# An edge-attention kernel: the edge and query projections laid out by edge instead of by feature and turned, with a looser tie of the gathers to TensorE

## The chip, the cores and the metric

The kernel runs on one core of one Trainium2 chip. The metric is the device time of one execution in microseconds (us). The parts of a core that matter here are TensorE (matrix products into PSUM, "PE" in the profile, its weight loads "PEld"), VectorE ("DVE"), ScalarE ("ACT"), GpSimd ("POOL", which here only issues indirect gathers), SyncE ("SP", which issues the plain DMAs) and the 16 DMA engines behind the queues.

## What is computed

A graph layer with 6,250 nodes of 128 features and 206,250 edges that are sorted by destination. With 8 heads of 16 features:

```python
Qh, Kh, Vh = h @ WQ, h @ WK, h @ WV          # per node, seen as (8, 16)
Eh = edge_attr @ WE                          # per edge
score = einsum('ehd,ehd,ehd->eh', Kh[src], Qh[dst], Eh) / 4
score = exp(clip(score, -5, 5))
wV = segment_sum(Vh[src] * score[:, :, None], dst)
Z = segment_sum(score, dst)
x = layernorm(x + wV / (Z[:, :, None] + 1e-06))
```

So each edge needs a product of three vectors (K of its source, Q of its destination, E of its own), a sum over each head's 16 features, an exponential, and a weighted V that is added into its destination.

## The kernel before

**Tiles and batches.** The edges are cut into 1,612 tiles of 128. A batch is four tiles (the last eight tiles make smaller ones), which gives 406 batches. A table of K and V by node (`kv`, 256 floats a row) and a table of Q (three bf16 parts of each row) are first written to DRAM by `table` and `q_rows`.

**What a batch does, engine by engine.**
- POOL gathers the rows of K and V of the batch's sources, one indirect DMA a tile (`gather`, line 307). The buffers are `kvrows`, GB = 17 of them.
- DVE makes two one-hot matrices (`stage_0`, line 337): `onehot` (edges on partitions, destination in a window on the free axis) for the final sum, and `onehotT` (126 rows of Q parts on partitions, edges on the free axis) to pick each edge's Q.
- PE picks Q with one bf16 product of 512 columns into `qps` (line 354). Features are then on partitions and edges on the free axis. ACT copies this to SBUF as `qT` (line 356). PE makes E in the same layout with one f32 product of 512 columns into `eps` (line 358); the profile counts an f32 product as two passes.
- DVE multiplies `qT` by `eps` into `eq` (`pairs`, line 365).
- PE turns the four 128x128 blocks of `eq` into `pps`, so that edges lie on partitions (`turn`, line 373).
- DVE multiplies the gathered K by `pps` (`kq`, line 379), sums over each head (`sc`, line 382) and clips (line 385). ACT takes the exponential twice, into a PSUM bank and into the last columns of `msg` (`weigh`, lines 391 and 393). DVE multiplies V by it (`messages`, line 413). PE adds the messages into `agg`, one f32 product a tile with `onehot` as the weights (`stage_c`, line 431). Every 11 tiles ACT copies `agg` to `sum` (line 441), and now and then PE joins the sums (`finish`), after which DVE norms a block of 128 nodes, one small instruction at each `fill()`.

**The order.** From batch 12 on the order of every engine is that of the program text (`manual_schedule`). In iteration b of the main loop (line 464) PE gets turn(b-1), the Q and E products of b, possibly a `finish`, and then agg(b-3). DVE gets kq, sc and clip of b-2, messages of b-3, the one-hots of b+2, and at the end `eq` of b. ACT gets qT(b), possibly `fin`, the exponentials of b-2, possibly `sum`.

**The tie.** POOL could run ahead as far as its buffers allow. From batch 16 on, line 318 makes the first gather of batch b wait for the Q product (`expanded`) of batch b - lag(b). The lag is 12 at batch 16 and falls by one every four batches down to STEP = 1 at batch 60. So later than that, gather(b) waits for the Q product of b-1.

**PSUM.** `eps` and `qps` have one bank each, `pps` two, `agg` two.

Of the kernel before, what the change touches and what calls it, by code (L numbers as in the profile page):

```python
# [8 lines left out]
F32 = mybir.dt.float32  # L9
I32 = mybir.dt.int32  # L10
BF16 = mybir.dt.bfloat16
AF = mybir.ActivationFunctionType
ALU = mybir.AluOpType
AX = mybir.AxisListType

P = 128
N, E, D, H, DH = 6250, 206250, 128, 8, 16
# [7 lines left out]
MW = D + H  # L25
B = 4
CH = 8
GB = 17
XB = 12
LOCK = XB + 4  # L30
STEP = 1
TAIL = 8
HEAD = 132
NG = (NT + G - 1) // G
AHEAD = 2
# [45 lines left out]
def edge_attention(ctx: ExitStack, tc: tile.TileContext, x, xT, srcT, dstT, dstB, dst0, bnd, lo, eaT,  # L81
# [30 lines left out]
    with ExitStack() as fast:  # L112
# [91 lines left out]
        ep = fast.enter_context(tc.tile_pool(name="edges", bufs=EB))  # L204
        wp = fast.enter_context(tc.tile_pool(name="work", bufs=3))
        sp = fast.enter_context(tc.tile_pool(name="sums", bufs=7))
        psE = fast.enter_context(tc.tile_pool(name="psE", bufs=1, space=bass.MemoryType.PSUM))
        psQ = fast.enter_context(tc.tile_pool(name="psQ", bufs=1, space=bass.MemoryType.PSUM))
        psP = fast.enter_context(tc.tile_pool(name="psP", bufs=2, space=bass.MemoryType.PSUM))
        psT = fast.enter_context(tc.tile_pool(name="psT", bufs=1, space=bass.MemoryType.PSUM))  # L210
        psA = fast.enter_context(tc.tile_pool(name="psA", bufs=2, space=bass.MemoryType.PSUM))
        psX = fast.enter_context(tc.tile_pool(name="psX", bufs=1, space=bass.MemoryType.PSUM))
# [1 line left out]
        bank = psX.tile([P, P + B * H], F32, name="bank")  # L214
        iota_p, exp_p = bank[:, :P], bank[:, P:].rearrange("p (b h) -> p b h", h=H)
        nc.vector.tensor_copy(iota_p, iota_f)

        def pair_bank(i, name, shape):

            pool, tag = ((psE, "eps"), (psP, "pps"), (psQ, "qps"), (psP, "pps"))[i % 4]  # L220
            return pool.tile(shape, F32, name=name, tag=tag)


        KB = 4
# [1 line left out]
        def table(b0):  # L226
            st = wp.tile([P, KB, 2 * D], F32, name="kvst", bufs=2)
            blocks = range(b0, min(NB, b0 + KB))
            for b in blocks:
                n = min(P, N - b * P)  # L230
                ps = pair_bank(b, "kvacc", [P, 2 * D])
                nc.tensor.matmul(ps[:n], xT_sb[:, LEFT + b * P:LEFT + b * P + n], wkv_sb,
                                 start=True, stop=True)
                if b % 2:
                    nc.vector.tensor_copy(st[:n, b - b0, :], ps[:n])
                else:
                    nc.scalar.copy(st[:n, b - b0, :], ps[:n])
            full = [b for b in blocks if (b + 1) * P <= N]
            if full:
                nc.sync.dma_start(  # L240
                    kv[b0 * P:(b0 + len(full)) * P].rearrange("(b p) f -> p b f", p=P),
                    st[:, :len(full), :])
            if len(full) < len(blocks):
                b = blocks[-1]
                nc.sync.dma_start(kv[b * P:N], st[:N - b * P, b - b0, :])
# [43 lines left out]
        def load_chunk(c):  # L289
            if c in chunks or c * CH >= NT:  # L290
                return
            n = min(CH, NT - c * CH) * P
            tl = ep.tile([P, CH * P], F32, name="ea")
            nc.sync.dma_start(tl[:, :n], eaT[:, c * CH * P:c * CH * P + n])
            chunks[c] = tl

        def ea_tiles(t, n):

            load_chunk(t // CH)
            j = t % CH * P  # L300
            return chunks[t // CH][:, j:j + n * P]

        def lag(b):

# [18 lines left out]
        def project(g, n):  # L323

            pt = psT.tile([P, B, P], F32, name="xtps", tag="oT")
            for i in range(n):
                nc.tensor.transpose(pt[:, i, :], g[:, i, :D], ident)
            xgT = wp.tile([P, B, P], F32, name="xgT", tag="kq", bufs=2)
            nc.scalar.copy(xgT[:, :n], pt[:, :n])
            for i in range(0, n, 2):  # L330
                k = min(2, n - i)
                pk = pair_bank(i // 2, "kvps", [P, 2, 2 * D])
                for j in range(k):
                    nc.tensor.matmul(pk[:, j, :], xgT[:, i + j, :], wkv_sb, start=True, stop=True)
                nc.scalar.copy(g[:, i:i + k, :], pk[:, :k, :])

        def stage_0(b):
            t0, n = batches[b][0], len(batches[b])
            oh = wp.tile([P, B, P], F32, name="onehot", bufs=AHEAD + 5)
            nc.vector.tensor_tensor(oh[:, :n], iota_p[:, None, :].to_broadcast([P, n, P]),  # L340
                                    rel[:, t0:t0 + n, None].to_broadcast([P, n, P]), op=ALU.is_equal)
            ohT = wp.tile([QROWS, B * P], BF16, name="onehotT", bufs=AHEAD + 2)
            e0 = t0 % RC * P
            nc.vector.tensor_scalar(ohT[:, :n * P], rels[t0 // RC][:, e0:e0 + n * P], node[:QROWS], None,  # L344
                                    op0=ALU.is_equal)
            st8[b] = oh, ohT

        def stage_a(b, g):
            t0, n = batches[b][0], len(batches[b])
            if b < XB:  # L350
                project(g, n)
            oh, ohT = st8.pop(b)
            pq = psQ.tile([P, B * P], F32, name="qps")
            expanded[b] = nc.tensor.matmul(pq[:, :n * P], loaded[t0 // WT], ohT[:, :n * P], start=True, stop=True)  # L354
            qT = wp.tile([P, B * P], F32, name="qT", bufs=2)
            nc.scalar.copy(qT[:, :n * P], pq[:, :n * P])  # L356
            pe = psE.tile([P, B * P], F32, name="eps")
            nc.tensor.matmul(pe[:, :n * P], we_sb, ea_tiles(t0, n), start=True, stop=True)  # L358
            st8[b] = [n, g, oh, pe, qT]

        def pairs(b):

            n, g, oh, pe, qT = st8[b]
            eq = wp.tile([P, B * P], F32, name="eq", bufs=2)
            nc.vector.tensor_tensor(eq[:, :n * P], qT[:, :n * P], pe[:, :n * P], op=ALU.mult)  # L365
            st8[b] = [n, g, oh, eq]

        def turn(b):

            n, g, oh, eq = st8[b]  # L370
            pp = psP.tile([P, B, D], F32, name="pps")
            for i in range(n):
                nc.tensor.transpose(pp[:, i, :], eq[:, i * P:i * P + P], ident)  # L373
            st8[b] = [n, g, oh, pp]

        def stage_b(b):
            n, g, oh, pp = st8[b]
            t1 = wp.tile([P, B, D], F32, name="kq", bufs=2)
            nc.vector.tensor_tensor(t1[:, :n], g[:, :n, :D], pp[:, :n], op=ALU.mult)  # L379
            fill()  # L380
            sc = wp.tile([P, B, H], F32, name="sc")
            nc.vector.tensor_reduce(sc[:, :n], t1[:, :n].rearrange("p b (h d) -> p b h d", h=H),  # L382
                                    axis=AX.X, op=ALU.add)
            fill()
            nc.vector.tensor_scalar(sc[:, :n], sc[:, :n], -20.0, 20.0, op0=ALU.max, op1=ALU.min)  # L385
            st8[b] = [n, g, oh, sc]

        def weigh(b):

            n, g, oh, sc = st8[b]  # L390
            nc.scalar.activation(exp_p[:, :n], sc[:, :n], AF.Exp, scale=0.25)  # L391
            m = wp.tile([P, B, MW], F32, name="msg")
            nc.scalar.activation(m[:, :n, D:], sc[:, :n], AF.Exp, scale=0.25)  # L393
            st8[b] = [n, g, oh, m]

# [62 lines left out]
        def fill():  # L458

            if norms and next(norms[0], None) is None:  # L460
                norms.pop(0)

        held = []
        for b in range(nbat + 4):
            if b >= XB and not manual:
                manual.append(fast.enter_context(tc.manual_schedule()))
            held += [(b + SLAG, store) for store in stores]
# [3 lines left out]
            if b < nbat:  # L471
                load_chunk(batches[b][0] // CH + EB - 3)
                load_rel(batches[b][0] // RC + 1)
                load_q(batches[b][0] // WT + QLOOK)
                g = gathered.pop(b) if b in gathered else gather(b)
                if b == min(XB, nbat - 1):
                    late_loads()
                if b == min(XB + 8, nbat - 1):
                    relative(C0, NT)
                if b == 14:  # L480
                    from_window(1)
                if b == 0:
                    for i in range(AHEAD):
                        stage_0(i)
                if b > 0:
                    turn(b - 1)
                stage_a(b, g)
            elif b == nbat:
                turn(b - 1)
            norms.extend(pending)  # L490
            pending.clear()
            for q in ready:
                finish(q)
            ready.clear()
            if 0 <= b - 2 < nbat:
                stage_b(b - 2)
            if 0 <= b - 3 < nbat:
                messages(b - 3)
            fill()
            if b + AHEAD < nbat:  # L500
                stage_0(b + AHEAD)
            if b < nbat:
                pairs(b)
            if 0 <= b - 2 < nbat:
                weigh(b - 2)
            if 0 <= b - 3 < nbat:
                stage_c(b - 3)
            fill()
            if b < nbat:
                while len(built) < q_built(min(NJ - 1, batches[b][0] // WT + QLOOK + 2)):  # L510
# [157 lines left out]
```

## Time and profile before

| | |
|---|---|
| runs | 2429.15, 2424.27, 2415.33 us; median 2424.27 |
| profiled execution | 2430.0 us, of which the traced span is 2428.1 us |
| TensorE clock granted, mean | 0.811 of full speed |
| busy: PE, PEld | 1539.8 us, 1086.0 us |
| busy: DVE | 1577.4 us |
| busy: ACT | 458.9 us |
| busy: POOL | 1534.0 us |
| DMA | 398.16 MB, mean 164 GB/s |
| chain that ended last | PE 34%, another core or an unknown queue 23%, DVE 19%, issue 16%, ACT 4% |

Busy time is the time in which an engine executes something; a row of the groups table gives the name of the tile that is written, what is read, the shapes, how often, the busy sum, the mean of one, and then the idle time of that engine just ahead of these instructions with the event that ended it. "issue" there is idle time for which the profile shows no wait. "remote", or "another core or an unknown queue", is a wait whose end the profile could not pair with an instruction. The starts of matmuls are recorded, their ends are modelled.

### The profile page before, as it was taken

What the parts mean: (1) busy time and instruction counts of PE and PEld (TensorE: products, weight loads), DVE (VectorE), ACT (ScalarE), POOL (GpSimd) and SP (SyncE); (2) the same over time, 40 slices, a digit from 0 to 9 for tenths busy, and PEclk for the clock granted to TensorE, in tenths of its full rate; (3) what the DMA queues carried; (4) which work ended last, traced back from release to release, by engine and by line L of the source; (5) the groups of instructions that cost most, each with busy time, mean ns of one, the idle gap of its engine ahead of it and who ended that gap; (6) DMA issues with size and microseconds to landing.
All of it is one profiled execution on the core that took longest, in us unless ns stands there. A gap on an engine that the chain in (4) does not pass through costs nothing.

```text
span 2428.1 us, 24930 instructions
## 1 busy us (share of the span) xinstructions
PE 1539.8 (63%) x6880; PEld 1086.0 (45%) x6880; DVE 1577.4 (65%) x3779; ACT 458.9 (19%) x1572; POOL 1534.0 (63%) x1619
## 2 busy tenths in 40 slices
PE   3587666666665666657666666666666656656665
PEld 2365444444444444444444444444444444444444
DVE  1368778666766666667667666666666667666766
ACT  0232122111111111111111111111111111111111
POOL 7346565666666666666666666666666666666664
PEclk6898898887878888778877878788778788887887
DMA  5645555556554555556456554655555556554642
GB/s 176 201 144 174 179 156 178 165 150 185 170 166 148 168 177 156 164 152 196 147 157 196 160 156 149 184 168 151 169 162 178 147 155 196 157 156 146 197 150 71
DMA packets 178482, 398.16 MB, mean 164 GB/s; under 512 B 61756, under 2 KB 87526, under 8 KB 178336
## 3 DMA queue, kind: packets, MB, share of 16 engines
q0 software_dynamic: 76592, 208.18, 29.4%
q1 hardware_dynamic: 100604, 187.38, 25.2%
q8 instruction: 57, 0.93, 0.2%
q10 hardware_dynamic: 1140, 0.93, 0.1%
q14 instruction: 89, 0.73, 0.1%
HBM read 381.54 MB, written 14.81 MB: 163 GB/s over the span
## 4 chain that ended last, share of the span: by engine, by line
PE 34%; another core or an unknown queue 23%; DVE 19%; issue 16%; ACT 4%; DMA 2%; POOL 1%; DVEq 1%; SPq 0%; ACTq 0%; POOLq 0%
PE agg L431 10%; PE eps L358 10%; PE pps L373 7%; DVE sc L382 4%; DVE kq L379 4%; DVE eq L365 3%; PE qps L354 3%; ACT qT L356 2%; DVE msg L413 2%; PE finps L401 2%; POOL kvrows L314 1%; DVE onehot L340 1%; DVE onehotT L344 1%; DMA kvrows<-kv,src 1%
## 5 line engine op out<-in xcount | busy, mean ns | idle before, releaser
L314 POOL DMA_INDIRECT kvrows<-kv,src x1564 | 1487.1, 951 | 862.3 <-issue 385.6
L431 PEld LDWEIGHTS agg<-msg,onehot 128*128 128x128 f32 x3224 | 516.7, 230 | 664.3 <-issue 520.9
L431 PE MATMUL agg<-msg,onehot 128*128 128x136 f32 x3224 | 560.5, 326 | 352.8 <-DVE msg L413 137.2
L373 PE MATMUL pps<-shift,eq 128*128 128x128 f32 x1612 | 320.5, 332 | 419.6 <-DVE eq L365 238.5
L365 DVE TENSOR_TENSOR eq<-qT,eps 128x512 f32<-128x512 f32 x406 | 276.4, 681 | 476.2 <-ACT qT L356 210.9
L358 PE MATMUL eps<-ea,we_sb 128*128 128x512 f32 (+1 forms) x812 | 528.2, 738 | 16.8 <-issue 13.4
L373 PEld LDWEIGHTS pps<-shift,eq 128*128 128x128 f32 x1612 | 221.4, 168 | 477.4 <-DVE eq L365 282.4
L356 ACT COPY qT<-qps 128x512 f32<-128x512 f32 x406 | 236.8, 583 | 1048.5 <-remote 428.8
L379 DVE TENSOR_TENSOR kq<-kvrows,pps 128x512 f32<-128x512 f32 x406 | 274.8, 677 | 12.1 <-remote 3.5
L413 DVE TENSOR_TENSOR msg<-kvrows,bank 128x512 f32<-128x512 f32 x406 | 274.6, 676 | 9.8 <-ACT bank L391 4.3
L382 DVE TENSOR_REDUCE sc<-kq 128x32 f32<-128x512 f32 x406 | 276.0, 680 | 7.3
L340 DVE TENSOR_TENSOR onehot<-bank,dst_sb 128x512 f32<-128x512 f32 x406 | 275.8, 680 | 0.0
L358 PEld LDWEIGHTS eps<-ea,we_sb 128*128 128x128 f32 x812 | 192.1, 238 | 50.0 <-issue 14.6
L354 PE MATMUL qps<-onehotT,qw 126*128 126x512 bf16 x406 | 187.3, 461 | 0.9 <-ACT qT L356 0.9
L344 DVE TENSOR_SCALAR onehotT<-relb,node 126x512 bf16<-126x512 bf16 x406 | 147.0, 363 | 16.7 <-remote 11.2
L391 ACT ACTIVATE bank<-sc 128x32 f32<-128x32 f32 x406 | 83.0, 204 | 257.2 <-DVE onehot L340 139.8
L401 PEld LDWEIGHTS finps<-sum,shift 128*128 128x128 f32 x478 | 73.1, 215 | 62.4 <-issue 33.9
L401 PE MATMUL finps<-sum,shift 128*128 128x136 f32 x478 | 75.8, 307 | 30.9 <-ACT sum L441 26.2
L262 DVE TENSOR_TENSOR qr<-qrows,qst 128x128 f32<-128x128 f32 (+1 forms) x49 | 14.2, 289 | 116.8 <-ACT qst L261 104.4
L393 ACT ACTIVATE msg<-sc 128x32 f32<-128x32 f32 x406 | 88.0, 217 | 0.0
L385 DVE TENSOR_SCALAR sc<-sc 128x32 f32<-128x32 f32 x406 | 79.2, 195 | 7.3
L441 ACT COPY sum<-agg 128x136 f32<-128x136 f32 x146 | 39.3, 269 | 236.2 <-remote 100.7
(66 smaller groups left out, 525.9 us busy)
## 6 DMA issues: line engine op xcount, KB each, us to landing
ea<-eaT SPq DMA_DIRECT2D x201, 512.0 KB
relb<-relD SPq DMA_DIRECT2D x100, 504.0 KB
kvrows<-kv,src POOLq DMA_INDIRECT x1564
qw<-qs SPq DMA_DIRECT2D x202, 31.5 KB
kv<-kvst SPq DMA_DIRECT2D x12, 512.0 KB
qs<-qst SPq DMA_DIRECT2D x48, 96.0 KB
xb<-x SPq DMA_DIRECT2D x48, 64.0 KB
out<-h SPq DMA_DIRECT2D x48, 64.0 KB
```

The costliest lines, as they stand in the source:

```text
L314: ins = nc.gpsimd.indirect_dma_start(out=g[:k, i, :f], out_offset=None, in_=rows, in_offset=bass.IndirectOffsetOnAxis(ap=src_col(t)[:k], a ...
L340: nc.vector.tensor_tensor(oh[:, :n], iota_p[:, None, :].to_broadcast([P, n, P]), rel[:, t0:t0 + n, None].to_broadcast([P, n, P]), op=ALU.i ...
L354: expanded[b] = nc.tensor.matmul(pq[:, :n * P], loaded[t0 // WT], ohT[:, :n * P], start=True, stop=True)
L356: nc.scalar.copy(qT[:, :n * P], pq[:, :n * P])
L358: nc.tensor.matmul(pe[:, :n * P], we_sb, ea_tiles(t0, n), start=True, stop=True)
L365: nc.vector.tensor_tensor(eq[:, :n * P], qT[:, :n * P], pe[:, :n * P], op=ALU.mult)
L373: nc.tensor.transpose(pp[:, i, :], eq[:, i * P:i * P + P], ident)
L379: nc.vector.tensor_tensor(t1[:, :n], g[:, :n, :D], pp[:, :n], op=ALU.mult)
L382: nc.vector.tensor_reduce(sc[:, :n], t1[:, :n].rearrange("p b (h d) -> p b h d", h=H), axis=AX.X, op=ALU.add)
L401: nc.tensor.matmul(ps, shift[:, P - s:2 * P - s], sums[k], start=i == 0, stop=stop and i == len(parts) - 1)
L413: nc.vector.tensor_tensor(m[:, :n, :D].rearrange("p b (h d) -> p b h d", h=H), g[:, :n, D:].rearrange("p b (h d) -> p b h d", h=H), exp_p[ ...
L431: nc.tensor.matmul(aggs[k], oh[:, i, :], m[:, i, :], start=first and not final, stop=last)
```

## The change

The two transposed products and the turn are replaced by products that give edges on partitions at once. For E, each tile's edge features are the weights and WE is the moving operand (four f32 products of 128 columns). For Q, each tile's part of `onehotT` is the weights and the loaded Q rows are the moving operand (four bf16 products of 128 columns). DVE then multiplies the gathered K by `qps` and the result by `eps`, both from PSUM. `pairs`, `turn`, `qT`, `eq` and `pps` go; `eps` and `qps` get two banks each. The pipeline is one iteration shorter: stage_b and the exponentials run on b-1, messages and agg on b-2. `onehot` has 9 buffers instead of 7, `onehotT` 6 instead of 4, `msg` 5 instead of 3, `kvrows` 15 instead of 17. The lag falls to STEP = 2.

```diff
-GB = 17
+GB = 15
-STEP = 1
+STEP = 2
...
-        psE = fast.enter_context(tc.tile_pool(name="psE", bufs=1, space=bass.MemoryType.PSUM))
-        psQ = fast.enter_context(tc.tile_pool(name="psQ", bufs=1, space=bass.MemoryType.PSUM))
-        psP = fast.enter_context(tc.tile_pool(name="psP", bufs=2, space=bass.MemoryType.PSUM))
+        psE = fast.enter_context(tc.tile_pool(name="psE", bufs=2, space=bass.MemoryType.PSUM))
+        psQ = fast.enter_context(tc.tile_pool(name="psQ", bufs=2, space=bass.MemoryType.PSUM))
...
-            oh = wp.tile([P, B, P], F32, name="onehot", bufs=AHEAD + 5)
+            oh = wp.tile([P, B, P], F32, name="onehot", bufs=AHEAD + 7)
-            ohT = wp.tile([QROWS, B * P], BF16, name="onehotT", bufs=AHEAD + 2)
+            ohT = wp.tile([QROWS, B * P], BF16, name="onehotT", bufs=AHEAD + 4)
...
-            pq = psQ.tile([P, B * P], F32, name="qps")
-            expanded[b] = nc.tensor.matmul(pq[:, :n * P], loaded[t0 // WT], ohT[:, :n * P], start=True, stop=True)
-            qT = wp.tile([P, B * P], F32, name="qT", bufs=2)
-            nc.scalar.copy(qT[:, :n * P], pq[:, :n * P])
-            pe = psE.tile([P, B * P], F32, name="eps")
-            nc.tensor.matmul(pe[:, :n * P], we_sb, ea_tiles(t0, n), start=True, stop=True)
+            pe = psE.tile([P, B, D], F32, name="eps")
+            for i in range(n):
+                nc.tensor.matmul(pe[:, i, :], ea_tile(t0 + i), we_sb, start=True, stop=True)
+            pq = psQ.tile([P, B, D], F32, name="qps")
+            for i in range(n):
+                expanded[b] = nc.tensor.matmul(pq[:, i, :], ohT[:, i * P:i * P + P], loaded[t0 // WT],
+                                               start=True, stop=True)
...
-        def pairs(b):
-            nc.vector.tensor_tensor(eq[:, :n * P], qT[:, :n * P], pe[:, :n * P], op=ALU.mult)
-        def turn(b):
-            for i in range(n):
-                nc.tensor.transpose(pp[:, i, :], eq[:, i * P:i * P + P], ident)
...
         def stage_b(b):
-            nc.vector.tensor_tensor(t1[:, :n], g[:, :n, :D], pp[:, :n], op=ALU.mult)
+            nc.vector.tensor_tensor(t1[:, :n], g[:, :n, :D], pq[:, :n], op=ALU.mult)
+            fill()
+            nc.vector.tensor_tensor(t1[:, :n], t1[:, :n], pe[:, :n], op=ALU.mult)
             fill()
...
-            m = wp.tile([P, B, MW], F32, name="msg")
+            m = wp.tile([P, B, MW], F32, name="msg", bufs=5)
...
-                if b > 0:
-                    turn(b - 1)
                 stage_a(b, g)
-            elif b == nbat:
-                turn(b - 1)
...
+            if 0 <= b - 1 < nbat:
+                stage_b(b - 1)
             if 0 <= b - 2 < nbat:
-                stage_b(b - 2)
-            if 0 <= b - 3 < nbat:
-                messages(b - 3)
+                messages(b - 2)
...
-            if b < nbat:
-                pairs(b)
-            if 0 <= b - 2 < nbat:
-                weigh(b - 2)
-            if 0 <= b - 3 < nbat:
-                stage_c(b - 3)
+            if 0 <= b - 1 < nbat:
+                weigh(b - 1)
+            if 0 <= b - 2 < nbat:
+                stage_c(b - 2)
```

In iteration b the orders are then: PE eps(b), qps(b), possibly `finish`, agg(b-2); DVE kq (twice), sc and clip of b-1, messages of b-2, the one-hots of b+2; ACT possibly `fin`, the exponentials of b-1, possibly `sum`.

## Prediction before the result

> **What bounds the kernel now.** I read the page first, then the groups with forms kept apart, then a window of the timeline, then POOL alone through the whole span. Busy shares name no engine: PE 63%, DVE 65%, POOL 63%. But POOL's row says more.
>
> ```profile
> L314 POOL DMA_INDIRECT kvrows<-kv,src x1564 | 1487.1, 951 | 862.3 <-issue 385.6
> ```
>
> One gather takes 951 ns and each is followed by 0.30 us of "issue", for which nothing else in the profile stands: back-to-back gathers start 1.25 us apart. All 1,612 (1,564 and 48 from x) at that pitch are 2,019 us of the 2,428 us. The rest of POOL's idle time is waiting. The timeline shows for what:
>
> ```profile
> 1210.00 0.38 PE L354 MATMUL qps<-onehotT,qw 126*128 126x512 bf16 x1
> ...
> 1211.72 1.17 PE L431 MATMUL agg<-msg,onehot 128*128 128x136 f32 x8 [0.48 <-issue]
> ...
> 1213.54 0.95 POOL L314 DMA_INDIRECT kvrows<-kv,src  x1 [0.30 <-issue]
> 1216.17 0.59 ACT L356 COPY qT<-qps 128x512 f32<-128x512 f32 x1 [6.82 <-remote]
> 1216.41 0.95 POOL L314 DMA_INDIRECT kvrows<-kv,src  x1 [1.91 <-remote]
> ```
>
> The Q product is recorded as run at 1210.0 to 1210.4, yet ACT, which waits for nothing but it, starts at 1216.17, and POOL, tied to the same product, at 1216.41. PE, DVE and ACT all stand still from 1212.9. So PE's completions were seen 5.8 us late, and only after POOL's last gather had ended at 1214.5. This is the usual state, as the waits of the engines show (us in total, times, longest):
>
> ```profile
> ACT qT L356 <- remote: 428.8, 89, 8.9
> ...
> POOL kvrows L314 <- issue: 399.9, 1306, 1.0
> ...
> POOL kvrows L314 <- remote: 221.7, 110, 2.7
> ```
>
> Going through POOL's timeline after 250 us, I count 158 stops longer than 0.6 us, 357 us in all, between runs of 4, 8 or 12 gathers, that is of one, two or three batches. After 440 us: 25 runs of 4 with a mean stop of 1.60 us, 28 of 8 with 1.88 us, 85 of 12 with 2.55 us. PE's completions arrive in time in the first 4 us or so of a run, later and later after it, and from 11 us on nearly always only when POOL has stopped. Why they are held I can't tell from this trace; that POOL's run goes with it, I can. The kernel is thus **gathers at a fixed pitch plus stops**, and a stop ends a run when POOL has used the batches that the tie of line 318 allows.
>
> **Sum, part by part** (against the profiled execution, 2430 us with a span of 2428; it lies 6 us above the median of the runs).
>
> *PE.* Warm, in the iteration from 1205.9: four turns at 0.109 us (0.44), Q 0.22, E two passes of 0.43 (0.86), agg eight passes of 0.116 (0.93): 2.45 us. Turns go: -0.44. E becomes eight passes of 128 columns; nearest row the turns, 0.109 each: 0.87, so +0.01. Q, four loads and four products of 128 columns, is not in the trace: at least 0.22 (as many columns), at most the turns' 0.44; I take 0.35, nearer the upper end since each brings a load: +0.13. Net -0.30 us, 120 us of PE's busy time in 406 batches. Cold (turns at 0.213 in the iteration from 1217.5) all doubles. None of it counts: PE waits in both cases, and its cover is POOL's 5.01 us a batch. If PE did bound, it would be worth the 120 us.
>
> A rule of the Trainium skill speaks against this part: "TensorE: Matmul & The Clock Gate", section "Back-to-back issue gap", gives about 81 ns a product at 128 columns and 131 at 512 in streams of loads and products. By it E would cost 8 x 81 instead of 2 x 131 ns, +0.39 us a batch or 157 us of PE's busy time; this trace's turns against its E passes (0.109 for 128 columns, 0.43 for 512) show cost by columns, so the row decides.
>
> *ACT.* The copy of qT goes, 406 x 0.583 = 237 us, off the path except as a link: Q to ACT to DVE to PE becomes Q to DVE.
>
> *DVE.* `eq` at 681 ns goes, a second multiply with one operand in PSUM comes: nearest row kq, 677 ns. It depends on the multiply ahead of it; the step from kq to sc, equally dependent, costs 0.03 us between: 12 us in all. DVE's five large instructions, 0.36 for onehotT and 0.18 for the clip stay 4.0 us a batch, under POOL's 5.01; uncovered 12 us.
>
> *Buffers and queues.* The one-hots' and `msg` buffers let DVE and ACT write while completions are held; 0 to -10 us, I take 0, as no wait of the onehot rows is large (0.0 us ahead of onehot, 16.7 ahead of onehotT). `kvrows` with 15: gather(b) needs the messages of b-15, and at the largest lag, 12, these precede in DVE's order what the tie already asks; 0, or one batch of POOL's time (5 us) where it bites. SP issues the same DMAs in the same places.
>
> *The tie and the loop*, the term that counts. Before, when a held run ends, PE has finished one Q product that POOL does not know of: qps(g+1) can't exist, since it stands behind turn(g), which waits for eq(g), which waits for ACT. So a release frees one batch of gathers at once. The next Q products follow 2.7 us later (1216.41 to 1219.07) and about 6.5 us later: they make runs of two and three. After the change two banks let PE finish Q of two batches while DVE waits for the first; with lag 2 a release frees **two batches at once**. The next Q product comes late, though. In PE's order it stands behind agg, which waits for messages. DVE needs two multiplies, sum, clip and messages first: 0.68 x 4 + 0.18, about 3.0 us. Then agg 1.0 to 1.8 and E with Q 1.2 to 2.5: at 5.2 to 7.3 us. Completions due 6 to 8 us into a run arrived within it four times in five (283 of 346 in my count), 1.5 us late; the new one must arrive before 10 us. One more is due at about 9.4, where 60% did, and serves if it arrives by 15. PE does more instructions ahead of these than before, so I take less: runs of two, three and four batches in the shares 0.4, 0.4, 0.2, a mean of 2.8. The 370 batches after 250 us then have 132 stops; at 0.4 x 1.88 + 0.6 x 2.55 = 2.28 us, 301 us instead of 357: **-56 us**. If every run had four batches: 93 x 2.55 = 237, -120 us. If every run had two with stops of 2.55: 185 x 2.55 = 472, +115 us; with stops of 1.88, 348, -9 us.
>
> *Start and end.* From 118 to 409 us POOL is slowed by the falling lag; PE does 54 batches there, 5.4 us each. The shorter loop takes perhaps 0.2 us off each: -10 (0 to -60 if DVE's 4.0 us became the bound). The end has one iteration less: -2 of the 15 us after the last gather.
>
> Sum: 2430 - 56 - 10 - 2 = 2362. As 6 us of that is this execution's excess over the median, while a single profile of the new kernel will scatter likewise, I leave it at **2362**.
>
> **Rivals.**
> 1. *POOL nearly unbroken.* If Q products arrive in time as often as before, four batches a run: 2430 - 120 - 10 - 2, about 2300. For it: PE no longer waits for ACT within a batch. Against it: Q comes last in its iteration.
> 2. *The same stops in another place.* DVE is now the one that waits for the held product, runs stay as they are, and only the end is shorter: 2424. For it: a run of 8 costs 0.94 us of stop a batch, one of 12 costs 0.85; length alone buys little.
> 3. *Slower: held completions grow with PE's instructions.* Late completions in unbroken runs arrive in multiples of 0.70 us (semaphore events of PE at 113.20, 114.61, 116.01 and 117.40 in the start-up run of 16 gathers), as if each instruction waited for its turn. A batch goes from 15 passes to 20. If no Q product due later than 5 us arrives within the run, every run has two batches. Before, the stop cost 357/370 = 0.965 us a batch; so runs of two turn to a loss when the stop exceeds 1.93 us, and held runs show 1.88 to 2.55. At 2.25 us: 370 x (1.125 - 0.965) = +59; against -12 of start and end: 2477. For it: the order agg, E, Q. Against it: the four in five above.
>
> **How the numbers follow.** Measurement of this kernel can tell about 0.5% from no change. Chances: the forecast (2335 to 2400) 0.42, unbroken 0.15, the same 0.15, slower 0.28. That gives faster 0.57, same 0.15, slower 0.28. The range takes in the unbroken case and the loss at a stop of 2.3 us: 2300 to 2490; beyond lie the stops of 2.55 us in runs of two and an E or Q that costs more than any row here.
>
> **What will show it.** Right: POOL's "issue" near 400 us as before, its other waits down by 50 to 70 us, no run of four gathers in the later part, runs of 8, 12 and 16; ACT busy near 222 us; PE busy lower, DVE as before. The E group at 3,224 passes of about 0.11 us pitch, the chain with "another core or an unknown queue" still large. Wrong: runs of 8 alone with stops over 2 us (rival 3); DVE waiting for landings of `kvrows` (the gathers themselves then bind); PE without idle time (the Q products cost more than 0.44 us).

## The result, and the profile after

The kernel after took 2433.98 us (median of 12 runs, 2422.64 to 2439.26), the kernel before beside it 2424.57 us (12 runs, 2415.33 to 2429.15). The ratio is 1.0037, with a 95% interval of [1.0021, 1.0053]: a change within 0.5%, where 2362 us had been forecast. The profiled execution of after has a span of 2420.9 us and is the fastest of its runs, so small differences of span between the two profiles say nothing.

From the page of the kernel after, the busy line and five rows of the groups (busy sum and mean ns of one, then the idle time ahead of them and what ended most of it):

```profile
PE 1402.2 (58%) x8886; PEld 1305.8 (54%) x8886; DVE 1601.0 (66%) x3779; ACT 244.4 (10%) x1166; POOL 1531.5 (63%) x1619
...
L308 POOL DMA_INDIRECT kvrows<-kv,src x1564 | 1484.5, 949 | 856.7 <-issue 385.4
L413 PE MATMUL agg<-msg,onehot 128*128 128x136 f32 x3224 | 645.7, 359 | 851.4 <-DVE msg L395 380.6
...
L349 PE MATMUL eps<-we_sb,ea 128*128 128x128 f32 x3224 | 575.3, 336 | 17.3 <-issue 16.0
L359 DVE TENSOR_TENSOR kq<-kvrows,qps 128x512 f32<-128x512 f32 x406 | 275.5, 679 | 439.5 <-remote 217.7
...
L352 PE MATMUL qps<-qw,onehotT 126*128 126x128 bf16 x1612 | 189.0, 247 | 11.6 <-issue 10.7
```

The rows of the kernel before that they are to be compared with, from its page (the row of its gathers stands in the prediction):

```profile
L431 PE MATMUL agg<-msg,onehot 128*128 128x136 f32 x3224 | 560.5, 326 | 352.8 <-DVE msg L413 137.2
...
L358 PE MATMUL eps<-ea,we_sb 128*128 128x512 f32 (+1 forms) x812 | 528.2, 738 | 16.8 <-issue 13.4
...
L379 DVE TENSOR_TENSOR kq<-kvrows,pps 128x512 f32<-128x512 f32 x406 | 274.8, 677 | 12.1 <-remote 3.5
...
L354 PE MATMUL qps<-onehotT,qw 126*128 126x512 bf16 x406 | 187.3, 461 | 0.9 <-ACT qT L356 0.9
```

PE and ACT do less, as meant: 138 and 215 us less busy than before. But POOL idles 856.7 us ahead of its gathers, where it was 862.3. The waits of after show who waits in ACT's old place (us in all, times, longest):

```profile
POOL kvrows L308 <- issue: 399.7, 1285, 4.1
PE agg L413 <- DVE msg L395: 380.6, 109, 10.8
DVE kq L359 <- remote: 217.7, 72, 6.3
POOL kvrows L308 <- remote: 216.7, 100, 2.8
```

`ACT qT <- remote`, 428.8 us before, is gone with its instruction. `DVE kq <- remote` has come (3.5 us before): DVE now waits for the held completion itself, and PE's agg waits for DVE's messages (137.2 us before, 380.6 after). POOL's waits for "remote" stand where they stood, 216.7 us against 221.7.

Counted in POOL's timeline in the prediction's way, after 250 us (stops are pauses over 0.6 us; a batch is four gathers):

| | runs | of 1, 2, 3 batches | mean run, batches | mean stop, us | stops, us |
|---|---|---|---|---|---|
| before | 159 | 34, 33, 89 | 2.31 | 2.24 | 356.8 |
| after | 173 | 30, 88, 53 | 2.12 | 2.06 | 357.0 |
| forecast | 132 | 0, 53, 53 (and 26 of four) | 2.8 | 2.28 | 301 |

A few runs of other lengths are in the totals alone. Many runs of three batches have become runs of two with a shorter stop, and the sum has not moved.

A stretch of after's timeline (start, duration, then engine, line and operation; idle time before it in brackets):

```profile
1206.55 0.69 DVE L359 TENSOR_TENSOR kq<-kvrows,qps 128x512 f32<-128x512 f32 x1 [3.73 <-remote]
1206.78 0.95 POOL L308 DMA_INDIRECT kvrows<-kv,src  x1 [2.01 <-remote]
...
1208.80 0.68 DVE L395 TENSOR_TENSOR msg<-kvrows,bank 128x512 f32<-128x512 f32 x1
...
1209.63 1.48 PE L413 MATMUL agg<-msg,onehot 128*128 128x136 f32 x8 [4.66 <-DVE vh L592]
...
1210.90 1.92 PE L349 MATMUL eps<-we_sb,ea 128*128 128x128 f32 x8
...
1212.61 0.63 PE L352 MATMUL qps<-qw,onehotT 126*128 126x128 bf16 x4
...
1215.56 0.95 POOL L308 DMA_INDIRECT kvrows<-kv,src  x1 [0.30 <-issue]
...
1217.01 0.95 POOL L308 DMA_INDIRECT kvrows<-kv,src  x1 [0.50 <-PE qps L352]
```

At 1206.5 a hold ends, and DVE and POOL start. PE waits for the messages until 1209.63, then does agg, E and, last, Q. So the next Q product is due (its recorded end) at 1213.24, 6.5 us into POOL's run; the next completion of PE is recorded only at 1216.75, after POOL has used its two batches (to 1216.51), and POOL goes on 0.50 us after its last gather instead of 0.30. Where the completion comes a little later, that is a stop. Over all runs after 440 us the first Q product of a run is due 5.33 us after the run's start (median), where it was 2.67 us before.

### The profile page after: what moved, and what is told of

Its sections match the earlier page's. It is cut to its first block, busy times and chain, and to the rows that moved or that the text cites. A ratio compares the mean times of both kernels' runs of the same rounds, so it can differ in the third digit from the quotient of the medians.

```text
span 2420.9 us, 28278 instructions
## 1 busy us (share of the span) xinstructions
PE 1402.2 (58%) x8886; PEld 1305.8 (54%) x8886; DVE 1601.0 (66%) x3779; ACT 244.4 (10%) x1166; POOL 1531.5 (63%) x1619
## 4 chain that ended last, share of the span: by engine, by line
DVE 38%; PE 19%; another core or an unknown queue 17%; issue 16%; DMA 4%; POOL 4%; ACT 2%; DVEq 0%; SPq 0%; ACTq 0%; POOLq 0%
PE agg L413 8%; DVE kq L361 8%; DVE kq L359 8%; DVE sc L364 7%; PE eps L349 6%; DVE msg L395 5%; POOL kvrows L308 4%; DMA kvrows<-kv,src 4%; DVE onehot L334 4%; DVE onehotT L338 2%; PE qps L352 2%; DVE sc L367 2%; PE finps L383 1%; PE kvps L328 1%
## 5 line engine op out<-in xcount | busy, mean ns | idle before, releaser
L308 POOL DMA_INDIRECT kvrows<-kv,src x1564 | 1484.5, 949 | 856.7 <-issue 385.4
L413 PE MATMUL agg<-msg,onehot 128*128 128x136 f32 x3224 | 645.7, 359 | 851.4 <-DVE msg L395 380.6
L413 PEld LDWEIGHTS agg<-msg,onehot 128*128 128x128 f32 x3224 | 558.3, 252 | 904.0 <-issue 865.1
L349 PE MATMUL eps<-we_sb,ea 128*128 128x128 f32 x3224 | 575.3, 336 | 17.3 <-issue 16.0
L359 DVE TENSOR_TENSOR kq<-kvrows,qps 128x512 f32<-128x512 f32 x406 | 275.5, 679 | 439.5 <-remote 217.7
L349 PEld LDWEIGHTS eps<-we_sb,ea 128*128 128x128 f32 x3224 | 545.2, 253 | 22.3 <-issue 20.3
L361 DVE TENSOR_TENSOR kq<-kq,eps 128x512 f32<-128x512 f32 x406 | 276.8, 682 | 10.9 <-remote 2.7
L352 PE MATMUL qps<-qw,onehotT 126*128 126x128 bf16 x1612 | 189.0, 247 | 11.6 <-issue 10.7
L352 PEld LDWEIGHTS <-onehotT 126*128 126x128 bf16 x1612 | 151.5, 114 | 26.9 <-issue 14.9
L226 PE MATMUL kvacc<-wkv_sb,xT_sb 128*128 128x256 f32 (+1 forms) x98 | 35.3, 505 | 45.3 <-issue 23.3
L308 POOL DMA_INDIRECT kvrows<-x,src x48 | 46.0, 959 | 16.5 <-issue 14.3
```

The lines of the kernel that those rows point to most:

```text
L308: ins = nc.gpsimd.indirect_dma_start(out=g[:k, i, :f], out_offset=None, in_=rows, in_offset=bass.IndirectOffsetOnAxis(ap=src_col(t)[:k], a ...
L349: nc.tensor.matmul(pe[:, i, :], ea_tile(t0 + i), we_sb, start=True, stop=True)
L352: expanded[b] = nc.tensor.matmul(pq[:, i, :], ohT[:, i * P:i * P + P], loaded[t0 // WT], start=True, stop=True)
L359: nc.vector.tensor_tensor(t1[:, :n], g[:, :n, :D], pq[:, :n], op=ALU.mult)
L361: nc.vector.tensor_tensor(t1[:, :n], t1[:, :n], pe[:, :n], op=ALU.mult)
L413: nc.tensor.matmul(aggs[k], oh[:, i, :], m[:, i, :], start=first and not final, stop=last)
```

## Experiments

There were six sets of runs; the kernels of a set share one chip and the runs of the kernel before. A ratio compares with that kernel in its own set. One fact has to be known to read them: only the comparison above and sets 2 and 5 show PE's completions held. ("Held" means: an instruction that waits for a PE product starts late, though the product has ended.) In sets 1, 3, 4 and 6 the kernel before takes 2043.11, 2043.60, 2049.40 and 2043.67 us, in sets 2 and 5 2449.92 and 2449.78 us. I call the former **unbroken** and the latter **held** sets. Sets 4 and 5 carry the same chip number, five minutes apart; as far as that number names a chip, the chip alone does not decide it. Each expectation states its theories itself; A, B and C have their meaning from set 3 on.

**Set 1 (unbroken): the tie and agg's place.** Edits: `STEP = 1` to `2` in the kernel before (e1); `STEP = 2` to `1` (e2) and to `4` (e3) in the kernel after; in e4, agg of one batch further back:

```diff
-        for b in range(nbat + 3):
+        for b in range(nbat + 4):
...
-            if 0 <= b - 2 < nbat:
-                stage_c(b - 2)
+            if 0 <= b - 3 < nbat:
+                stage_c(b - 3)
```

> The kernel before with STEP = 2 alone. Theory of tickets (a run of gathers ends when POOL has used the batches that the tie allows; a looser tie makes the runs one batch longer): runs of 8, 12 and 16 gathers instead of 4, 8 and 12 after 440 us, about 100 stops of 2.5 us instead of 140 with 310 us in sum, ratio about 0.975. Rival (the pace is set by how late PE's completions come in the loop through PE and DVE; a longer run only delays them further): the stops' sum stays within 20 us, ratio 1.00.

> The changed kernel with STEP = 1, so that the products and buffers change alone. Theory of tickets: most runs one batch shorter, runs of 4 and 8, stops of 1.6 to 2 us a run, sum of the stops after 440 us up from 320 to about 420 us, ratio to before about 1.04. Rival (the tie doesn't matter): ratio within 1.00 to 1.01.

> The changed kernel with STEP = 4. Theory of tickets: runs of at least 16 gathers, about 75 stops of 2.6 us after 440 us, sum about 200 us instead of 320, ratio about 0.955. Rival (the loop through PE and DVE sets the pace): POOL just runs two batches further ahead once, and then stops as often; ratio 1.00, or above it where completions are held longer.

> The changed kernel with the sum into agg one iteration later (agg of b-3 instead of b-2 in PE's order), so that the E and Q products no longer stand behind messages of the iteration before. Theory (Q comes too late in the run because it stands behind agg): the next Q product is done 2.5 to 3 us after a release instead of 6 to 7, runs of 12 and 16 take the place of runs of 8, sum of the stops after 440 us down from 320 to about 240 us, ratio about 0.97. Rival (what holds completions is the number of PE instructions in a run, wherever they stand): runs of 8 stay, ratio 1.00.

| | median, us | ratio | 95% interval |
|---|---|---|---|
| e1 | 2043.45 | 1.0003 | [0.9994, 1.0013] |
| e2 | 2217.27 | 1.0862 | [1.0843, 1.0880] |
| e3 | 2047.54 | 1.0019 | [1.0009, 1.0028] |
| e4 | 2045.31 | 1.0012 | [1.0002, 1.0021] |

In e1 all 1,612 gathers start 1.255 us apart without one stop, from 3.4 to 2026.5 us. From the groups of e1:

```profile
L314 POOL DMA_INDIRECT kvrows<-kv,src x1564 | 1486.1, 950 | 476.5 <-issue 365.0
...
L356 ACT COPY qT<-qps 128x512 f32<-128x512 f32 x406 | 236.3, 582 | 529.4 <-PE qps L354 528.7
```

The gather takes 950 ns here as in the kernel before's profile (951); the idle time ahead of gathers is 476.5 us instead of 862.3. ACT's wait ends with the Q product and no longer with "remote". After 440 us ACT's copy starts more than 0.3 us after both the end of its Q product and the end of ACT's work before it in 161 of 341 batches of the kernel before, up to 7.9 us; in e1 in none of 319 (at most 0.04 us). So the first half of the prediction's picture holds: the kernel is gathers at a fixed pitch plus stops, and the stops come with late completions. The 172 stops of the kernel before are 432.6 us over its whole span; less the 0.30 us that follow every gather anyway, 52 us in all, they are the 381 us between 2424.57 and 2043.11. e1 itself tests neither of its theories, since nothing was held; e3 and e4 could not gain for the same reason.

e2 shows what the looser tie is for. The timeline of e2:

```profile
1000.76 0.39 PE L352 MATMUL qps<-qw,onehotT 126*128 126x128 bf16 x4
...
1003.37 0.69 DVE L359 TENSOR_TENSOR kq<-kvrows,qps 128x512 f32<-128x512 f32 x1 [3.74 <-DMA kvrows<-kv,src]
...
1006.49 2.15 PE L413 MATMUL agg<-msg,onehot 128*128 128x136 f32 x8 [5.34 <-DVE msg L395]
...
1008.44 1.92 PE L349 MATMUL eps<-we_sb,ea 128*128 128x128 f32 x8
...
1010.15 0.63 PE L352 MATMUL qps<-qw,onehotT 126*128 126x128 bf16 x4
...
1011.05 0.94 POOL L308 DMA_INDIRECT kvrows<-kv,src  x1 [3.32 <-PE qps L352]
```

DVE waits for the rows of one batch, PE for its messages, Q stands behind agg and E, and POOL waits 3.32 us for Q: from one Q product to the next 9.4 us pass here, without any held completion. In the new order Q is behind the messages, and a tie of one batch costs 8.6% by that alone. Both of e2's theories missed this: 1.04 and at most 1.01.

**Set 2 (held): the tie again, and agg's place.** f1 is the kernel after, f2 has `STEP = 4`, f3 has that and e4's edit, f4 is the kernel before with `STEP = 12`.

> The changed kernel as it is, beside the kernel before, on the chip of this call. In the earlier call's place the kernel before took 2043 us and PE's completions came at most 0.23 us late; where the change was measured it took 2425 us and half of them came over 1 us late. Theory (two regimes: with late completions the stops of the gathers decide, without them the gather pitch alone): where the kernel before takes about 2043 us, the ratio is 1.00 within 0.3% and there is one run of gathers; where it takes about 2425 us, 1.00 to 1.005 with runs of 8. Rival (the change only happens to cancel in one of the two): a ratio over 1.01 or under 0.99 in the other.

> The changed kernel with STEP = 4. Without late completions: 1.00. With late completions: theory of tickets: runs of at least 16 gathers, about 75 stops of 2.6 us after 440 us, ratio about 0.955; rival (the loop through PE and DVE sets the pace, POOL only runs two batches further ahead once): stops' sum within 20 us of 320 us, ratio 1.00 or above.

> The changed kernel with agg of b-3 instead of b-2 in PE's order and STEP = 4. Without late completions: 1.00. With late completions: theory (the order agg, E, Q delays the product that POOL and DVE wait for): clearly below the run with STEP = 4 alone, ratio about 0.93 to 0.95; rival (number of PE instructions in a run): no difference to STEP = 4 alone.

> The kernel before with STEP = 12, the lag that it starts with, so the tie never tightens. Without late completions: 1.00. With late completions: theory of tickets: POOL runs ahead until its buffers or the tie stop it, after that it goes on at the pace of PE, whose completions are held longest in long runs; the gain is the ramp alone, ratio 0.97 to 1.00. Rival (stops are what costs, so fewer are better): ratio below 0.95. Third possibility (unbroken gathers hold completions so long that PE and DVE starve): ratio above 1.02.

| | median, us | ratio | 95% interval | mean run, batches | stops after 250 us, us |
|---|---|---|---|---|---|
| f1 | 2456.25 | 1.0029 | [1.0013, 1.0045] | 1.86 | 398.8 |
| f2 | 2458.79 | 1.0037 | [1.0024, 1.0050] | 1.89 | 400.9 |
| f3 | 2443.17 | 0.9964 | [0.9948, 0.9980] | 2.10 | 376.5 |
| f4 | 2463.38 | 1.0053 | [1.0038, 1.0068] | 2.00 | 379.2 |

f1 repeats the result. (f4 also ends later: 52.3 us after its last gather, where the kernel before has 15.1.) The theory that the tie of two batches ends the runs falls: a tie of four (f2) or twelve (f4, in the old order) lengthens no run and makes nothing faster. What a release frees is what PE and DVE have done, and they stand still while completions are held: counted after 440 us by the ends of the Q products, f2 starts a run with two batches free in 106 of 172 cases and with one in 65, in spite of its tie of four. f4's 1.0053 lies in none of the three ranges of its expectation. With agg out of Q's way (f3 against f2) 0.7% comes back: the first Q product of a run is due 3.75 us after its start instead of 6.70 us. That is the direction of f3's theory, but far less than the 0.93 to 0.95 it gave.

**Set 3 (unbroken).** g1 is the kernel before with its E and Q products cut as the change cuts them, values unchanged:

```diff
-            expanded[b] = nc.tensor.matmul(pq[:, :n * P], loaded[t0 // WT], ohT[:, :n * P], start=True, stop=True)
+            for i in range(n):
+                expanded[b] = nc.tensor.matmul(pq[:, i * P:i * P + P], loaded[t0 // WT], ohT[:, i * P:i * P + P],
+                                               start=True, stop=True)
...
-            nc.tensor.matmul(pe[:, :n * P], we_sb, ea_tiles(t0, n), start=True, stop=True)
+            ea = ea_tiles(t0, n)
+            for i in range(n):
+                nc.tensor.matmul(pe[:, i * P:i * P + P], we_sb, ea[:, i * P:i * P + P], start=True, stop=True)
```

g2 is the kernel after with one E product a batch, of the first tile alone, so it leaves out the E of three tiles; g4 moves one call of the kernel after; g3 is g4 with Q ahead of E in `stage_a` and `STEP = 3`:

```diff
-            for i in range(n):
-                nc.tensor.matmul(pe[:, i, :], ea_tile(t0 + i), we_sb, start=True, stop=True)
+            ea_tile(t0 + n - 1)
+            nc.tensor.matmul(pe[:, :n, :], ea_tile(t0), we_sb[:, None, :].to_broadcast([P, n, D]), start=True, stop=True)
```
```diff
-            if 0 <= b - 1 < nbat:
-                stage_b(b - 1)
             if 0 <= b - 2 < nbat:
                 messages(b - 2)
+            if 0 <= b - 1 < nbat:
+                stage_b(b - 1)
```

> The kernel before with E and Q each cut into four products of 128 columns, same values: 16 products of PE in a batch (12 after the change), 21 passes of 128 columns in place of 2 of 512 for E. Theory A (each PE instruction that is issued adds to the time for which completions are held): slower than before by at least 1%, 1.01 to 1.03, with more stops of POOL. Theory B (what counts is how soon after a release the next Q product is due, and whether it gets through before the hold sets in): 0.998 to 1.005, stops of POOL within 20 us of those of before in the same call's manner (430 to 450 us). If the chip shows no held completions (one unbroken run of gathers), 1.000 by both, and the run tells nothing.

> The kernel after with E as one product of 512 columns a batch in place of four of 128: the weights are those of the batch's first tile and the four tiles get the same E values, so three tiles' E is left out; the columns that PE streams are as many. Nine products a batch instead of twelve. Theory A: faster than the kernel after by 1% or more, that is 0.985 to 0.995 of before. Theory B: as the kernel after, 1.000 to 1.006 of before, since Q stands where it stood.

> The kernel after with DVE's messages of b-2 ahead of the two multiplies of b-1, Q's products ahead of E's, and a tie of three batches. Theory B: the next Q product is due about 2 us after a release instead of 5 to 7, gets through within the run, and runs get longer: 0.98 to 0.993 of before, stops down by 15 to 50 us. Theory A: nothing gained, 1.000 to 1.006. Rival C (a hold comes with the length of POOL's run whatever is due, so each release costs its stop and the number of hand-offs from PE that a batch needs sets how many): 0.995 to 1.005.

> The kernel after with one thing moved: DVE's messages of b-2 stand ahead of the multiplies of b-1, so that they and PE's agg can be done while DVE would wait for a held Q product. Theory B: Q is due 2.5 to 3.5 us after a release: 0.985 to 0.995 of before, fewer runs of two batches and more of three. Theory A: 1.000 to 1.006. Rival C: 0.997 to 1.005. Against g3, theory B allows g3 another 0 to 0.5%.

(In g1 E's passes go from 2 to 8 a batch; the 21 in its expectation is a slip.) Measured: g1 0.9998 [0.9989, 1.0007], g2 1.0019 [1.0010, 1.0028], g3 1.0016 [1.0007, 1.0025], g4 1.0031 [1.0019, 1.0042]. With gathers nearly unbroken (at most six runs, 7 us of stops), little that PE or DVE does reaches the end: the edit of the kernel before costs nothing, the kernels in the new order lose 0.2 to 0.3%. These runs do not tell A, B and C apart.

**Sets 4 (unbroken), 5 (held) and 6 (unbroken): the same kernels again.**

> The same kernel as g1, again, for a chip on which POOL's gathers are stopped by held completions (on the chip of g1 they ran unbroken). Theory A (each further PE instruction lengthens the hold): 1.01 to 1.03 of before. Theory B (what counts is how soon after a release the next Q product is due): 0.998 to 1.005.

> The same kernel as g4, again, for a chip with held completions. Theory B: 0.985 to 0.995 of before, with fewer runs of two batches and more of three. Theory A: 1.000 to 1.006. Rival C (every release costs its stop, whatever is due): 0.997 to 1.005.

> The same kernel as g1 and h1, again, for a chip with held completions. In the traces so far a train of held completions begins with the first completion of a burst of PE work (the turns in the kernel before, E in the kernel after: 38 and 40% of them), seldom with a later one (Q after E: 9%). Theory A (each further PE instruction lengthens the hold): 1.01 to 1.03 of before. Theory B (the place of the completions counts): 0.998 to 1.005, since the bursts keep their places.

> The same kernel as g4 and h4, again, for a chip with held completions. Theory B: 0.985 to 0.995 of before, with fewer runs of two batches and more of three. Theory A: 1.000 to 1.006. Rival C (every release costs its stop, whatever is due): 0.997 to 1.005.

> The same kernel as g2 (E as one product of 512 columns a batch, the four tiles get the E of weights from the first, three tiles' E is left out), again, for a chip with held completions. k1 showed that more and narrower products cost 1.0% in the kernel before; if the number of products sets this in the new order too (theory A), three fewer of twelve bring 0.3 to 0.8%: 0.995 to 1.000 of before, against 1.003 of the kernel after. If only the place counts (theory B), 1.001 to 1.006. On a chip without held completions 1.000 to 1.003.

> The same kernel as g3 (messages first, Q ahead of E, a tie of three), again, for a chip with held completions. k4 (messages first alone) gave 0.9926 of before. Theory B: Q is due about 0.9 us sooner, so as k4 or up to 0.5% better, 0.987 to 0.994. If the first completion of a burst is the one that is held whichever it is (Q would be it), nothing more is gained: 0.992 to 0.998. Longer runs as in k4: more runs of three batches than after the change. On a chip without held completions 1.000 to 1.003.

| | median, us | ratio | 95% interval | mean run, batches | stops after 250 us, us |
|---|---|---|---|---|---|
| h1 | 2047.33 | 0.9994 | [0.9984, 1.0004] | nearly unbroken | |
| h4 | 2055.26 | 1.0033 | [1.0021, 1.0046] | unbroken | |
| **k1** | 2474.64 | **1.0102** | [1.0079, 1.0125] | 1.89 | 419.0 |
| **k4** | 2431.51 | **0.9926** | [0.9903, 0.9948] | 2.34 | 368.8 |
| n2 | 2049.14 | 1.0023 | [1.0014, 1.0033] | nearly unbroken | |
| n3 | 2049.23 | 1.0023 | [1.0014, 1.0033] | nearly unbroken | |

k4 settles one thing, k1 only half of another. k1's edit, more and narrower products, costs 1.0% in the kernel before, at the lower end of A's range, though the same edit costs nothing in the unbroken sets (g1, h1). From k1's groups:

```profile
L362 PE MATMUL eps<-ea,we_sb 128*128 128x128 f32 x3224 | 600.7, 345 | 2.0 <-ACT kvrows L335 1.7
L358 ACT COPY qT<-qps 128x512 f32<-128x512 f32 x406 | 236.4, 582 | 1245.8 <-remote 685.9
```

ACT's wait for held Q products rises from 428.8 us before to 685.9. Of POOL's runs after 440 us, 162 of 175 have two batches: the picture of rival 3. More than the number of products changes, though. A run's first Q product is due as early as before (2.66 us, before 2.67), its second 0.56 us later (7.21, 6.65). And of the completions due 6 to 9 us into a run, only 94 of 354 arrive within it (283 of 346 before). The last share depends on the run's length too, so it shows that fewer arrive, not that the number of products is the cause by itself. And the edit moves a signal, which its expectation overlooked ("the bursts keep their places"): in k1's trace the turns signal their end in 7 of 406 batches (397 before), so the Q product is the first completion that a burst of PE work signals. By the semaphore events (the profile's record of when a completion was counted) it is the first to be held, with those behind it, in 198 of 343 cases, where before it was in 60 of 341. Whether the number of products or this place cost the 1.0% is open.

k4 moves one call and beats both kernels. From its timeline:

```profile
1205.12 1.87 PE L349 MATMUL eps<-we_sb,ea 128*128 128x128 f32 x8 [1.01 <-issue]
...
1205.51 0.94 POOL L308 DMA_INDIRECT kvrows<-kv,src  x1 [2.82 <-remote]
...
1205.82 0.69 DVE L395 TENSOR_TENSOR msg<-kvrows,bank 128x512 f32<-128x512 f32 x1 [4.96 <-ACT bank L373]
1206.42 0.68 DVE L359 TENSOR_TENSOR kq<-kvrows,qps 128x512 f32<-128x512 f32 x1
...
1206.78 0.63 PE L352 MATMUL qps<-qw,onehotT 126*128 126x128 bf16 x4
...
1207.21 2.13 PE L413 MATMUL agg<-msg,onehot 128*128 128x136 f32 x8
```

Q is due at 1207.41, 1.9 us after POOL's run began, and is recorded at 1207.65; agg comes behind it. Over all runs the first Q is due 2.81 us after the start, and runs of three batches are 69 where f1 has 15. The intervals of f1 and k4 lie apart: 1.0029 against 0.9926, about 1.0% of 2450, 25 us (each against its own set's kernel before; the kernel after itself was not run in k4's set). Rival C (0.997 to 1.005, the order counts for nothing) falls, and k4 lies in B's range. n2, which was to show whether the number of products also costs in the new order, and n3 fell into an unbroken set; both stay untested under held completions.

## Why the prediction was wrong

The term that counts was to bring 56 us and brought nothing: the stops after 250 us are 357.0 us for 356.8. The measured 2433.98 us lies between the prediction's bounds only because these took in the loss of rival 3 as well.

*What bounds the kernel*: right. e1 shows the same gather at the same pitch without the stops.

**The step that failed is the term of the tie and the loop, -56 us**: "a release frees two batches at once", with runs of two, three and four batches in the shares 0.4, 0.4, 0.2, a mean of 2.8. The due times in it were near: 5.2 to 7.3 us for the next Q product and about 9.4 for the one after, measured medians 5.33 and 8.70 (f1: 6.78 and 9.58). Two things failed. First, a release did not always free two batches. By the ends of the Q products, after 440 us, two batches were free at the start of 74 of 153 runs and only one at 78 (before: one at all 138), as the second Q product had often not ended by then; 30 of the 173 runs after 250 us have one batch. Second, the chance that the next product is seen in time was carried over from the kernel before, "four times in five" (the 283 of 346 behind it are the completions due 6 to 9 us into a run, not 6 to 8; the share is the same). After the change 217 of 315 such completions arrived (f1: 126 of 367), counted by events, so roughly. Of the 74 runs that began with two batches 38 reached a third; before, 85 of 138 that began with one did. No run had four. The mean was 2.12 instead of 2.8, and the sum of stops 357.0 us instead of 301. The price of a stop was close (2.06 us for 2.28).

Where the gain went, by the runs: ACT's link in the loop is gone, and Q's place behind agg, which waits for messages, took its gain back. That part is shown: 16 us by f3 against f2 in one set, 25 us by k4 against f1 across two sets. The further products may be a second part, which is not shown. k1 has six more products a batch in the old order and costs 25 us; the change has two more in all, so a third of it, some 8 us, is an estimate from k1 (14 us if PE's passes count, 5 more for k1's 9), and k1's loss may come from its moved signal instead. The remaining 40 to 45 us of the 78 between forecast (-68) and result (+10) have no experiment of their own: even k4, with Q early, reached runs of 2.34 batches and not 2.8.

*PE*: its busy sum fell by 138 us for 120 forecast, at a lower clock (0.779 for 0.811). The prices of the parts were off. At nearly the same clock (0.806) k1's E in eight passes cost 600.7 us for 528.2, 0.18 us a batch for the 0.01 taken; in g1, with its clock near e1's, 0.07. Q in four cost 196.3 for 187.3 us, 0.02 us a batch for the 0.13 taken. The estimate from the Trainium skill, "TensorE: Matmul & The Clock Gate", section "Back-to-back issue gap", was +0.39 us a batch for E; neither run shows that much. Nothing of this reached the end by PE's busy time: PE idles 1,019 us of after's span.

*ACT* fell by 215 us (237 forecast), off the path. *DVE* rose by 24 (12 forecast), hidden. *Start*: POOL reached batch 60 at 401.0 us for 409.0 before, the -10 of the forecast; but f1 has 412.1, so a single profile cannot settle it. *End*: 15.5 us after the last gather for 15.1, no gain where -2 was taken. *Buffers*: taken as 0, not tested apart.

*The rivals.* The second, "the same stops in another place", is nearest to what came: 2424 forecast (2430 - 2 = 2428 by the sum's own base), and DVE waits where ACT waited, though the runs did not stay as they were. The third, the slower one, did not decide the sign, though its two conditions are half there: runs of two became the commonest (88 of 173), but with stops of 1.90 us after them, just under the 1.93 from which it was to turn to a loss. k1 shows the loss when a mean stop of 2.16 us goes with such runs; that the hold grows with the number of PE's instructions, as this rival has it, no run shows. Of the prediction's signs of being right, POOL's "issue" near 400 us came (399.7); but runs of one batch stayed (24 of 155 after 440 us), and runs of four did not come.

## What to carry to other kernels

When completions come late, ask of each order when the product that frees the next transfer is due after a release, and what it stands behind: here, dropping ACT from the loop gained nothing, as the product then queued behind one that waits for DVE's work. Letting DVE do what it already can (the messages of the batch before) ahead of an instruction that may wait gave 0.9926 (k4) where the kernel after has 1.0029 (f1, in another set). A chance of arrival counted in one order of the work did not carry over to another. And before lags are read from semaphore events, count whether the events are all there: in the held profiles they are not, and the starts of the waiting instructions are the safer measure.

## What was not expected of the hardware

The same kernel takes 2043 to 2049 us in four sets and 2424 to 2450 in the comparison and the other two, and the difference is POOL's stops, which come with late completions of PE. The clearest pair is one kernel in both conditions, k4 (held) and h4 (unbroken). After 440 us, 137 of 339 first gathers of a batch in k4 start more than 0.3 us after both their Q product had ended and POOL was ready, up to 2.8 us; in h4 none of 320 does (at most 0.04 us). The granted clock is lower in k4 as well (0.756 for 0.829), but these starts are counted from the product's end. DVE's completions are not late: in the kernel before, PE starts the turns at most 0.06 us after `eq` and PE's own work before it have ended, in all 342 batches after 440 us. Where POOL stops, what is held is let go some 2 us after its last gather has ended (mean stop 2.24 us before, 2.06 after). The Trainium skill, "TensorE: Matmul & The Clock Gate", section "The cost: per-tile semaphore tail", says that such increments follow one another at about 26 ns each; that is far too little for these lags, and no run here shows what holds them.

The held profiles have a second mark: many of their semaphore events are missing, from every engine. The kernel before has 1,937 events of DVE's semaphore where e1 has 3,727, 938 of ACT's for 1,573, 1,338 of PE's for 1,625, and 5,408 of the gathers' eight semaphores for 25,730. All eight held profiles are like this; in the twelve unbroken ones next to none is missing. In 143 of the 342 batches above the turns start before the event that they wait for is on record. So lags and arrivals that are read from events (the counts of completions that arrived, here and in the prediction, and its steps of 0.70 us, which do not occur in e1) are rough; the starts of instructions do not depend on it. Whether the recording itself has a share in the holds no run here shows, and what decides between the two conditions was not found.

A hold begins most often at the first completion of a burst of PE work. Counted from the events after 440 us (a lag over 0.3 us, with the completion before it already seen), E, which comes first, begins a hold in 145 of 340 cases after the change, Q behind it in 45 of 340; before, the turns in 127 of 342 and Q in 60 of 341. In k1, where Q is the first to signal, it is Q in 198 of 343. That points to the place in the burst rather than to the product that stands there; whether Q ahead of E in the new order would only move the hold to Q is open, since n3 met no held completions.
